# Factorization machine layer: inputs laid out by halves and loaded in fewer pieces

## The chip, the cores and the metric

The kernel runs on one core of a Trainium2 chip. The metric is device time in microseconds (us), the median of several executions. A core has five engines with a queue each: TensorE (PE in the profile, its weight loads are PEld), VectorE (DVE), ScalarE (ACT), GpSimd (POOL) and SyncE (SP). SyncE only issues transfers here; ScalarE and GpSimd issue some too. All transfers are carried out by the core's 16 DMA engines.

## The reference

For a batch x of 1024 rows with 512 features, a weight of shape (64, 512, 512), a linear weight of shape (512, 512) and a bias of 512:

```python
out_lin = x @ lin_w.T + lin_b
xv = jnp.einsum('bf,efm->bem', x, weight)
zp = jnp.einsum('bf,efm->bem', jnp.square(x), jnp.square(weight))
interaction = 0.5 * jnp.sum(jnp.square(xv) - zp, axis=1)
return out_lin + interaction
```

Everything is float32. By far the largest part is xv, 64 products of 1024 x 512 x 512.

## The kernel before

The matrix products are done by Strassen's scheme (Winograd's form), seven products of quarter matrices instead of eight, on two levels. The outer level splits x in four quarters: A11 and A12 are the first 512 rows with one and the other half of the features (k = 0, 1 and k = 2, 3 below), A21 and A22 the other 512 rows. Of these the kernel makes R5 = A22 - A21, R6 = -R5 - A11, R7 = A11 - A21 and R3 = -R6 - A12, and from each of the seven the inner level's sums. All of them stay in one tile, x_all, for the whole run. Then 16 groups of the weight pass by; in each, seven trees (one for each outer product) of seven inner products run on TensorE (`tree`, L603; its matmuls are at L625), while VectorE, ScalarE and GpSimd make the sums of weights and collect the results from PSUM.

Ahead of the groups stands the linear layer, x @ lin_w.T, with one level of the same scheme (`lin_product`, L442; its matmuls are at L458). It runs in the head, while the first inputs arrive. Its seven products come in the order 1, 2, 4, 5, 6, 3, 7. Product 1 (A11 with the first quarter of lin_w) and product 2 (A12) go by k: a feature index is p*4 + k for partition p and k from 0 to 3, so each k is a slab of 128 features, and each slab can be multiplied when it has landed. Product 1 takes k = 0 and 1, product 2 takes k = 2 and 3, and each slab goes by halves of its 512 rows. Product 4 takes A22 and t4, a sum of quarters of lin_w (`column_sums`, L430: t1, t2, t4, t3 in that order on VectorE; t1 and t2 need the second half of lin_w's columns). Product 5 is the first that needs R5, and so A21.

The inputs arrive on two queues. `load_x` (L348) issues pieces of x from SyncE into the tiles oa0 (A11), oa1 (A12), oa2 (A21) and oa3 (A22); `load_lw` (L355) issues pieces of lin_w from the queue that it is given into ob0 (k = 0, 1) and ob1 (k = 2, 3), by halves of the columns (c = 0, 1). In DRAM x is stored transposed, (512, 1024), and so is lin_w: a feature's row of x is 4 KB long, and 2 KB of it belong to one half of the batch. After the inputs SyncE issues the first group's weights w11, w21, w12, w22a (L339).

The order of the work on each engine is written by a planner (`Plan`, L21 to L194) when the kernel is built: each operation has a cost, reads and writes; TensorE's order is given by keys; the other engines take what is ready and most urgent in a simulated time. The loads of the head aren't planned: they are issued as the code has them, and `landing` (L345) only tells the planner at what time, by estimate, their data is there. The compiled program gives each transfer of SyncE and ScalarE one of eight completion semaphores in turn, and a transfer that gets one for the second time first waits until the earlier one has landed.

Later, from the second group to the eighth, `x_squares` (L726) loads quarters of x once more, to square them.

Of the kernel before, what the change touches and what calls it, by code (L numbers as in the profile page):

```python
# [197 lines left out]
def kernel(  # L198
# [38 lines left out]

    nc = tc.nc
    NG, NQ, _, NCB, KH, N = weight.shape
    B = xT.shape[1]  # L240
    M = out.shape[0]
    NB = B // P
    NK = 2 * KH
    MG = M // NG
    MI = MG // 4
    E = N // MI
    H = B // 2
    Q = B // 4

# [10 lines left out]
    buf = {}  # L260
# [32 lines left out]
    bias = sb.tile([P, M // P], F32, tag="bias", name="bias")  # L293
    w2_sum = sb.tile([P, NK, M], F32, tag="w2_sum", name="w2_sum")
    acc_dram = dram.tile([P, M // P, B], F32, tag="accd", name="accd")
    lin_dram = dram.tile([P, M // P, B], F32, tag="lind", name="lind")
    sq_dram = dram.tile([P, 7, 7, Q], F32, tag="sqd", name="sqd")
# [22 lines left out]
    def act(o, i, func, reads, writes, cost=1.04):  # L320
        def emit(_):
            if func is None:
                nc.scalar.copy(o, i)  # L323
            else:
                nc.scalar.activation(o, i, func)  # L325

        plan.add({ACT: cost}, emit, reads, writes)
# [10 lines left out]
    def dma(o, i, reads, writes, move=1.75, on=(SP,)):  # L338
        plan.add(dict.fromkeys(on, 0.45), lambda e: queues[e].dma_start(o, i), reads, writes,  # L339
                 land=2.0, move=move)  # L340


    x_src = xT.rearrange("(p k) b -> p k b", k=NK)
    lw_src = lin_wT.rearrange("(p k) m -> p k m", k=NK)
    def landing(name, at):  # L345
        plan.add({SP: 0.0}, None, (), (name,), land=at - 2 * plan.HOP)

    def load_x(h, k, lo, hi, at):  # L348

        n, r = f"oa{2 * h + k // KH}", k % KH  # L350
        nc.sync.dma_start(buf[n][:, r, lo * Q:hi * Q], x_src[:, k, h * H + lo * Q:h * H + hi * Q])  # L351
        for u in range(lo, hi):
            landing((n, r, u), at)

    def load_lw(queue, ks, c, at):  # L355

        l, r = f"ob{ks[0] // KH}", ks[0] % KH
        queue.dma_start(  # L358
            buf[l][:, r:r + len(ks), ts(c, N // 2)],
            lw_src[:, ks[0]:ks[0] + len(ks), ts(c, N // 2)],  # L360
        )
        for k in ks:
            landing((l, k % KH, c), at)

    load_x(0, 0, 0, 1, 3.5)
    load_lw(nc.scalar, [0], 0, 3.5)
    load_x(0, 0, 1, 2, 3.9)
    load_lw(nc.scalar, [1], 0, 5.2)
    load_x(0, 1, 0, 2, 5.0)
    load_lw(nc.scalar, [2, 3], 0, 7.2)  # L370
    load_x(0, 2, 0, 2, 6.4)
    load_x(0, 3, 0, 2, 7.4)
    load_lw(nc.sync, [0, 1], 1, 8.4)
    load_lw(nc.sync, [2, 3], 1, 9.2)
    for at, k in enumerate((2, 3, 0, 1)):
        load_x(1, k, 0, 2, 10.0 + 0.8 * at)
    nc.scalar.dma_start(bias[:], lin_b)
    landing("bias", 9.5)
    nc.scalar.preload_act_table(AF.Square)


    zero = nc.const_aps.tensor(0.0, [P, N])
# [23 lines left out]
    def x_sum(writes, o, a, b, kind, reads, size, engine=DVE):  # L406

        if kind != "-a - b":
            costs, emit = two_input(engine, o, a, b, kind == "a - b", size)
        else:  # L410
            costs = two_input(DVE, o, a, b, True, size)[0]

            def emit(_):
                nc.vector.scalar_tensor_tensor(o, a, -1.0, b, ALU.mult, ALU.subtract)

        plan.add(costs, emit, reads, writes, both=engine == DVE)
# [285 lines left out]
    def turn(g, tiles, half=True):  # L702

        row = tuple((acc_name[g], i, pos) for i, pos in acc_parts if (i in (2, 3)) + 2 * (i in (4, 5)) & tiles)
        b = {1: slice(0, NB // 2), 2: slice(NB // 2, NB), 3: slice(0, NB)}[tiles]
        a, t = buf[acc_name[g]][:, b, :], buf["turned"][:, b, :]
        size = (b.stop - b.start) / NB
        names = tuple(("turned", h) for h in range(2) if tiles & 1 << h)
        if half:
            plan.add({ACT: 0.2 + 0.25 * size}, lambda _: nc.scalar.mul(a, a, 0.5), row, row)  # L710
        plan.add(
            {DVE: 0.1 + 0.27 * size},
            lambda _: nc.vector.transpose(
                t.rearrange("p n m -> p (n m)"), a.rearrange("p n m -> p (n m)")
            ),
            row, names,
        )
        return b, names
# [7 lines left out]
    def x_squares(i):  # L726

        a, b = c_ring(), c_ring()
        quads = {"A11": (0, 0), "A12": (0, 1), "A21": (1, 0), "A22": (1, 1)}

        def take(o, n):
            if n in raw_dram:
                dma(buf[o], raw_dram[n], (("rawd", n),), (o,))
            else:
                h, q = quads[n]
                dma(buf[o], x_src[:, ts(q, KH), ts(h, H)], (), (o,))
                act(buf[o], buf[o], AF.Square, (o,), (o,), 1.07)

        one, two, kind = {
            1: ("A11", None, None), 2: ("A12", None, None), 4: ("A22", None, None),  # L740
            5: ("A21", "A22", "a + b"), 6: (5, "A11", "a - b"), 7: ("A11", "A21", "a - b"),
            3: ("A12", 6, "a - b"),
        }[i]
        take(a, one)
        if two:
            take(b, two)
            x_sum((a,), buf[a], buf[a], buf[b], kind, (a, b), 1024)
        if i in raw_dram:
            dma(raw_dram[i], buf[a], (a,), (("rawd", i),))
        slots = sq_dram[:, i - 1, 0:4, :].rearrange("p (k q) b -> p k (q b)", k=2)  # L750
        if i in (3, 4, 7):
            return dma(slots, buf[a], (a,), (("sqd", i),))
        a11, a21, a12, a22 = (buf[a][:, k, ts(q, Q)] for k in range(2) for q in range(2))
        s1, s2, s4 = (buf[b].rearrange("p k b -> p (k b)")[:, ts(z, Q)] for z in range(3))
        for o, x, y, kind, to in (
            (s1, a21, a22, "a + b", (b,)),
            (s2, s1, a11, "a - b", (b,)),
            (s4, a12, s2, "a - b", (b,)),
            (a21, a11, a21, "a - b", (a,)),
        ):  # L760
            x_sum(to, o, x, y, kind, (a, b), Q)
        dma(slots, buf[a], (a,), (("sqd", i),))
        dma(sq_dram[:, i - 1, 4:7, :].rearrange("p s b -> p (s b)"),
            buf[b].rearrange("p k b -> p (k b)")[:, 0:3 * Q], (b, ("sqd", i)), (("sqd", i),), 1.3)
# [26 lines left out]
    for g in range(NG - 1):  # L791
        group(g)
        b, names = turn(g, 3)
        m, c = (g * MG) % P, g * MG // P
# [183 lines left out]
    v, o2, u2, f = ("w12", 0), ("w12", 1), ("T1", 0), ("T1", 1)  # L978
# [96 lines left out]
    for i in (7, 4, 3):  # L1075
        if i != 3:
            at = {7: 5, 4: 4}[i]
# [5 lines left out]
    for h in (1, 0):  # L1083
        b, names = turn(last, 1 + h, h == 1)
# [3 lines left out]
    for u, bank in ((1, b2[0]), (0, "b3")):  # L1088
        o = buf[bank][:, u, :]
# [9 lines left out]
    for u, lo, hi, bank, key in ((1, 0, H, "b1", 9.7), (0, 0, Q, b2[1], 14), (0, Q, H, b2[0], 15)):  # L1099
        o = buf[bank][:, 0, 0:hi - lo]  # L1100
# [41 lines left out]
```

## Time and profile before

| | |
|---|---|
| Median of 3 runs | 1403.36 us (1403.36 to 1403.88) |
| The profiled execution | 1404.54 us, of which span 1402.7 us |
| TensorE | 1396.1 us busy, 3296 matmul instructions |
| VectorE, ScalarE, GpSimd | 1093.5, 711.5, 1050.2 us busy |
| Transfers | 211.33 MB, 151 GB/s on average |
| Loads of x in the head, from SyncE | 7 of 256 KB, 2 of 128 KB |
| Loads of lin_w in the head | 3 from ScalarE, 2 from SyncE |

The span goes from the first to the last instruction; the time of an execution lies some 1.8 us above it. A matmul in float32 appears as two instructions with two weight loads. The chain that ended last is followed back from the last instruction, at each step to what released it. An entry such as `[1.32 <-DMA oa<-xT]` says that the engine was idle for 1.32 us before the instruction, and that a transfer from xT into oa ended it. The bound of a stage is read from what ends its waits, not from how busy an engine is over the whole.

### The profile page before, as it was taken

What the parts mean: (1) busy time and instruction counts of PE and PEld (TensorE: products, weight loads), DVE (VectorE), ACT (ScalarE), POOL (GpSimd) and SP (SyncE); (2) the same over time, 40 slices, a digit from 0 to 9 for tenths busy, and PEclk for the clock granted to TensorE, in tenths of its full rate; (3) what the DMA queues carried; (4) which work ended last, traced back from release to release, by engine and by line L of the source; (5) the groups of instructions that cost most, each with busy time, mean ns of one, the idle gap of its engine ahead of it and who ended that gap; (6) DMA issues with size and microseconds to landing.
All of it is one profiled execution on the core that took longest, in us unless ns stands there. A gap on an engine that the chain in (4) does not pass through costs nothing.

```text
span 1402.7 us, 10645 instructions
## 1 busy us (share of the span) xinstructions
PE 1396.1 (100%) x3296; PEld 626.6 (45%) x3296; DVE 1093.5 (78%) x971; ACT 711.5 (51%) x748; POOL 1050.2 (75%) x741
## 2 busy tenths in 40 slices
PE   9999999999999999999999999999999999999998
PEld 4444444444444444444444444444444444444454
DVE  7978696877959778696877959678696877959676
ACT  4546373544736456373544636355373544636444
POOL 4796786958778686786958678686786958678994
PEclk9999999999999999999999999999999999999999
DMA  6674573827649285582827538184472817538363
GB/s 224 165 180 131 124 195 105 230 86 178 200 121 239 85 196 170 125 227 78 228 56 180 154 96 209 45 196 122 127 180 81 227 53 180 153 97 207 101 165 114
DMA packets 54999, 211.33 MB, mean 151 GB/s; under 512 B 21472, under 2 KB 23008, under 8 KB 33056
## 3 DMA queue, kind: packets, MB, share of 16 engines
q0 software_dynamic: 12320, 83.24, 30.8%
q1 hardware_dynamic: 40352, 125.12, 25.3%
q10 hardware_dynamic: 2272, 2.30, 0.5%
q8 instruction: 27, 0.44, 0.1%
q14 instruction: 28, 0.23, 0.1%
HBM read 180.75 MB, written 12.45 MB: 138 GB/s over the span
## 4 chain that ended last, share of the span: by engine, by line
PE 98%; DMA 1%; DVE 0%; ACTq 0%; SPq 0%; DVEq 0%; issue 0%
PE b L625 96%; PE b L458 1%; PE b L936 1%; PE b L1055 1%; DMA ob<-lin_wT 0%; DMA oa<-xT 0%; DVE x_all L311 0%; ACTq L358 0%; SPq L351 0%; DVE T L1034 0%; DVEq L1138 0%; DVE T L1067 0%; DVEq L311 0%
## 5 line engine op out<-in xcount | busy, mean ns | idle before, releaser
L625 PE MATMUL b<-t,x_all 128*128 128x512 f32 x1792 | 806.0, 592 | 0.0
L625 PEld LDWEIGHTS b<-t,x_all 128*128 128x128 f32 x1792 | 340.4, 190 | 427.0 <-issue 420.7
L625 PE MATMUL b<-w,x_all 128*128 128x512 f32 x768 | 358.1, 592 | 0.0
L311 POOL TENSOR_TENSOR t<-w 128x512 f32<-128x512 f32 x128 | 171.9, 1344 | 150.2 <-PE b L625 77.8
L323 ACT COPY p<-b 128x1024 f32<-128x1024 f32 x163 | 164.0, 1006 | 179.3 <-PE b L625 178.5
L625 PEld LDWEIGHTS b<-w,x_all 128*128 128x128 f32 x768 | 145.9, 190 | 183.7 <-issue 182.5
L311 POOL TENSOR_TENSOR t<-w,t 128x512 f32<-128x512 f32 x128 | 175.3, 1370 | 56.7 <-PE b L625 56.5
L325 ACT ACTIVATE oa<-oa 128x1024 f32<-128x1024 f32 x124 | 129.7, 1057 | 145.0 <-DVE oa L311 145.0
L625 PE MATMUL b<-T,x_all 128*128 128x512 f32 x384 | 180.4, 592 | 0.0
L323 ACT COPY b<-b 128x1024 f32<-128x1024 f32 x113 | 112.7, 997 | 133.0 <-PE b L625 132.5
L332 DVE TENSOR_REDUCE acc<-oa 128x16 f32<-128x1024 f32 x124 | 148.8, 1211 | 36.8 <-ACT oa L325 36.8
L332 DVE TENSOR_REDUCE w_sum<-wsq 128x16 f32<-128x1024 f32 x128 | 153.7, 1209 | 3.2 <-ACT wsq L325 3.2
L311 DVE TENSOR_TENSOR oa<-b,p 128x1024 f32<-128x1024 f32 x95 | 115.8, 1219 | 37.2 <-PE b L625 37.2
L325 ACT ACTIVATE c<-c 128x1024 f32<-128x1024 f32 x77 | 79.6, 1055 | 124.3 <-DVE c L311 82.2
L311 POOL TENSOR_TENSOR t<-T 128x512 f32<-128x512 f32 x64 | 86.4, 1350 | 56.6 <-issue 30.9
L625 PEld LDWEIGHTS b<-T,x_all 128*128 128x128 f32 x384 | 73.0, 190 | 91.8 <-issue 90.9
L311 DVE TENSOR_TENSOR p<-b,p 128x1024 f32<-128x1024 f32 x79 | 96.4, 1220 | 20.9 <-PE b L625 16.9
L311 DVE TENSOR_TENSOR ob<-b,p 128x1024 f32<-128x1024 f32 x48 | 58.6, 1222 | 65.8 <-PE b L625 65.8
L325 ACT ACTIVATE wsq<-w 128x1024 f32<-128x1024 f32 x96 | 98.2, 1053 | 12.0 <-DMA w<-weight 9.2
L311 POOL TENSOR_TENSOR t<-T,t 128x512 f32<-128x512 f32 x64 | 82.8, 1293 | 17.8 <-PE b L625 17.7
L311 POOL TENSOR_TENSOR c<-oa,p 128x1024 f32<-128x1024 f32 x32 | 84.7, 2647 | 0.0
L311 DVE TENSOR_TENSOR oa<-b,oa 128x1024 f32<-128x1024 f32 x62 | 75.6, 1219 | 9.5 <-PE b L625 9.5
(100 smaller groups left out, 1394.0 us busy)
## 6 DMA issues: line engine op xcount, KB each, us to landing
w<-weight SPq DMA_DIRECT2D x48, 1024.0 KB, 5.0
T<-weight POOLq DMA_DIRECT2D x45, 1024.0 KB, 9.0
T<-weight SPq DMA_DIRECT2D x30, 1024.0 KB, 6.9
w<-weight POOLq DMA_DIRECT2D x16, 1024.0 KB, 11.1
w<-T POOLq DMA_DIRECT2D x16, 1024.0 KB, 7.0
w22a<-weight SPq DMA_DIRECT2D x8, 1024.0 KB, 10.9
w22b<-weight SPq DMA_DIRECT2D x8, 1024.0 KB, 10.9
c<-xT SPq DMA_DIRECT2D x9, 512.0 KB, 6.1
```

What stands on the lines that cost most here:

```text
L311: f(o, a, b)
L323: nc.scalar.copy(o, i)
L325: nc.scalar.activation(o, i, func)
L332: lambda _: nc.vector.tensor_reduce(o, i.rearrange("p a (m e) -> p a m e", e=E), axis=AX.X, op=ALU.add),
L458: nc.tensor.matmul(buf[bank][:, c, rows], b[:, k, ts(c, P)], a[:, k, rows], start=first and k == 0 and rows.start == 0, stop=k == KH - 1, ...
L625: nc.tensor.matmul(buf[b][:, j, :], buf[f"X{i}"][:, SLOT[p], ts(j, P)], op, start=first, stop=True, skip_group_check=True,)
L936: nc.tensor.matmul(buf[b][:, u, lo:lo + Q], tt[i][p][0], buf[f"X{square_at[i]}"][:, SLOT[p], :], start=first and not lo, stop=True, skip_g ...
L1055: nc.tensor.matmul(o, ap[:, k, ts(u, P)], in_rows(o, buf[raw[i]][:, k, lo:hi]), start=first and k == 0, stop=k == 1, skip_group_check=True,)
```

## The change

x and lin_w are laid out differently in DRAM, on the host: as [half, partition, k, row], where a half is 512 rows of x (or 256 columns of the transposed lin_w). A partition's two k's of one half then lie side by side, and one transfer takes both with rows of 4 KB for x and 2 KB for lin_w. k = 2 and 3 of the first half of x become one load, and the second half of x becomes two (A22, then A21) instead of four. The second half of lin_w's columns is still loaded in two transfers, but from ScalarE's queue, behind the bias and the load of ScalarE's function table; SyncE then issues x alone. The estimates of landing given to the planner change with it. `x_squares` reads from the new layout.

```diff
-    def load_x(h, k, lo, hi, at):
+    def load_x(h, ks, lo, hi, at):
 
-        n, r = f"oa{2 * h + k // KH}", k % KH
-        nc.sync.dma_start(buf[n][:, r, lo * Q:hi * Q], x_src[:, k, h * H + lo * Q:h * H + hi * Q])
-        for u in range(lo, hi):
-            landing((n, r, u), at)
+        n, r = f"oa{2 * h + ks[0] // KH}", ks[0] % KH
+        nc.sync.dma_start(
+            buf[n][:, r:r + len(ks), lo * Q:hi * Q],
+            xT[h][:, ks[0]:ks[0] + len(ks), lo * Q:hi * Q],
+        )
...
+    def load_lw(ks, c, at):
+
+        for q in sorted({k // KH for k in ks}):
+            mine = [k for k in ks if k // KH == q]
+            r = mine[0] % KH
+            nc.scalar.dma_start(
+                buf[f"ob{q}"][:, r:r + len(mine), ts(c, N // 2)],
+                lin_wT[c][:, mine[0]:mine[0] + len(mine), :],
+            )
...
-    load_x(0, 0, 0, 1, 3.5)
-    load_lw(nc.scalar, [0], 0, 3.5)
-    load_x(0, 0, 1, 2, 3.9)
-    load_lw(nc.scalar, [1], 0, 5.2)
-    load_x(0, 1, 0, 2, 5.0)
-    load_lw(nc.scalar, [2, 3], 0, 7.2)
-    load_x(0, 2, 0, 2, 6.4)
-    load_x(0, 3, 0, 2, 7.4)
-    load_lw(nc.sync, [0, 1], 1, 8.4)
-    load_lw(nc.sync, [2, 3], 1, 9.2)
-    for at, k in enumerate((2, 3, 0, 1)):
-        load_x(1, k, 0, 2, 10.0 + 0.8 * at)
+    load_x(0, [0], 0, 1, 3.5)
+    load_lw([0], 0, 3.5)
+    load_x(0, [0], 1, 2, 4.2)
+    load_lw([1], 0, 4.2)
+    load_x(0, [1], 0, 2, 5.2)
+    load_lw([2, 3], 0, 5.8)
+    load_x(0, [2, 3], 0, 2, 7.2)
     nc.scalar.dma_start(bias[:], lin_b)
-    landing("bias", 9.5)
+    landing("bias", 7.2)
+    load_x(1, [2, 3], 0, 2, 9.8)
+    load_x(1, [0, 1], 0, 2, 11.5)
     nc.scalar.preload_act_table(AF.Square)
+    load_lw([0, 1, 2, 3], 1, 8.8)
...
-                dma(buf[o], x_src[:, ts(q, KH), ts(h, H)], (), (o,))
+                dma(buf[o], xT[h][:, ts(q, KH), :], (), (o,))
...
+    def halves(a):
+
+        a = np.asarray(a)
+        return np.ascontiguousarray(a.reshape(2, a.shape[0] // 2, p, n_k).transpose(0, 2, 3, 1))
+
     arrays = {
-        "xT": np.ascontiguousarray(np.asarray(r_x).T),
+        "xT": halves(r_x),
...
-        "lin_wT": np.ascontiguousarray(np.asarray(L0_rec_lin_w).T),
+        "lin_wT": halves(L0_rec_lin_w),
```

## The prediction

> **What bounds the kernel now.** I read the page's first lines, then the waits of TensorE over the whole span, then the chain that ended last, and last the first 17 us engine by engine.
>
> ```profile
> span 1402.7 us, 10645 instructions
> PE 1396.1 (100%) x3296; PEld 626.6 (45%) x3296; DVE 1093.5 (78%) x971; ACT 711.5 (51%) x748; POOL 1050.2 (75%) x741
> ```
>
> TensorE has work throughout. Its complete list of waits in the whole run has three entries:
>
> ```profile
> PE b L458 <- DMA oa<-xT: 1.3, 1, 1.3
> PE b L384 <- PEq L1131: 0.8, 1, 0.8
> PE b L458 <- DVE x_all L311: 0.7, 1, 0.7
> ```
>
> Two of them are at L458, the matmuls of the linear layer, so both lie in the head. The 0.8 is the start of the program. The chain, in order of time, shows where the head ends (start, length, what; pieces left out at "..."):
>
> ```profile
> 1.67 6.55 DMA ob<-lin_wT
> 8.22 0.02 issue
> 8.24 0.34 SPq L351
> ...
> 9.10 6.12 DMA oa<-xT
> 15.21 0.03 issue
> ...
> 15.34 1.24 DVE x_all L311
> 16.57 0.04 issue
> 16.62 12.28 PE b L458 x28
> 28.90 1.72 PE b L625 x4
> 30.62 1.72 PE b L458 x4
> 32.33 1323.55 PE b L625 x3084
> ```
>
> From 16.62 us on the chain is TensorE back to back until 1398.03: 1381.4 us in which loads don't matter as long as they keep their cover. The end of the run is therefore 16.62, the start of product 5 (the first that needs R5 = A22 - A21), plus a constant. Only what moves that start counts. TensorE up to there (start, busy, instructions, idle before):
>
> ```profile
> 3.48 2.25 PE L458 MATMUL b<-oa,ob 128*128 128x256 f32 x8
> 7.04 5.42 PE L458 MATMUL b<-oa,ob 128*128 128x256 f32 x24 [1.32 <-DMA oa<-xT]
> 12.30 3.60 PE L458 MATMUL b<-oa,p 128*128 128x512 f32 x8
> 16.62 7.13 PE L458 MATMUL b<-x_all,p 128*128 128x512 f32 x16 [0.72 <-DVE x_all L311]
> ```
>
> k-step 0 is done at 5.73; k-step 1 waits for x's k=1 (landed 6.91); k=1, 2, 3 run until 12.2 (24 x 0.215); product 4 runs 12.30 to 15.73 (8 x 0.429). Then 0.89 us without work (the view says 0.72, its ends being modelled). Two holes, 1.31 and 0.89: 2.2 us in all. That is the whole stake, 0.16%.
>
> Why A21 is late is in the queue's own waits:
>
> ```profile
> SPq L351 <- DMA ob<-lin_wT: 3.8, 2, 3.0
> ```
>
> [...] The second load of x's second half thus waited 3.0 us for lin_w's [2,3], which landed at 8.22; the last two went out at 8.62 and 9.06. The trace's completion records of the last (A21's k=1): fifteen of its sixteen engines had landed by 12.74, the sixteenth at 15.21.
>
> **What the Trainium skill says.** "DMA: Bandwidth & Descriptors", section "Why a DMA increments its semaphore by 16 and not by 1": a transfer is finished when all its engines are. The 12.74 against 15.21 agrees. Section "Queues, rings and completion order": an engine takes the rings in turns by packets, and descriptors of one ring start in order, so what lies ahead on the same ring is paid first; lin_w's [2,3], third on its queue, took 6.6 us beside x's pieces, which agrees. Section "Why small descriptors are slow (HBM only)": a fixed cost per packet. The packet records agree: 1 KB took 46 ns, 2 KB 84, 8 KB 309, that is 37 ns per KB and about 9 per packet. Section "Issuing engines are not separate DMA queues": moving a load between queues saves issue time only; here 0.33 to 0.47 us each.
>
> **The change part by part.**
>
> Longer rows. Per engine (8 of the 128 rows of each transfer): before 16x46 ns for the two first pieces of x, 7x8x84 for the others, 64x46 for lin_w: 0.74+4.70+2.94 = 8.38 us. After: 0.74 + 8x84 + 3x8x159 for x (4 KB: 84 plus 2x37 = 158 to 159, an estimate from the three sizes), and 16x46 + 24x84 for lin_w: 0.74+0.67+3.82+0.74+2.02 = 7.98. So 0.40 us less wire, all before A21's end.
>
> Issue. SyncE issued 11 transfers before the weights, now 6. Four go at 0.75 to 2.5 (0.43 each). A22 is now the ninth and waits for lin_w's first (landed 3.34): out at 3.36 instead of 4.71 and 8.24. A21 waits for the third of x's and lin_w's first four (3.87): out at 3.9 instead of 8.62 and 9.06. The 3.0 us wait is gone from x and falls on w11, now the thirteenth, which waits for lin_w's [2,3]. Before, w11 went out at 9.57 and landed at 17.98; TensorE's first use is at 28.7, through a sum on GpSimd that starts at 18.05 and takes under 2 us, so some 8 us of cover. I count it as nothing; a weight later than that would cost the excess.
>
> A21's landing. A21's first half landed at 12.10 before, with 7.7 us of packets ahead of and in it: 12.10-1.5-7.7 = 2.9 us over pure packet time (first packet 1.5; waits, slow first reads, receipt). The same on 7.98: 1.5+7.98+2.9 = 12.4. Below: 10.2[...]; above: 14.9 if one engine lags by 2.5 again. Needed: product 4's end 15.73 less R5's 1.24 and 0.09 of hops = 14.4. At 12.4, R5 waits for VectorE instead: its sums of lin_w, then the 1.22 us addition into ob2 that ended at 13.79; so R5 13.8 to 15.05, product 5 at 15.73. **The hole of 0.89 goes.**
>
> k-step 1. x's k=1 keeps its place, third on SyncE's queue, and its issue time. lin_w's [2,3] beside it moves 2 KB packets instead of 1 KB: in turns, 8x(84+84) = 1.34 instead of 8x(84+46) = 1.04, so up to 0.3 later; with both started earlier by nothing, at best as much earlier as less queueing gives. From -0.4 (it landed on twelve engines by 5.38) to +0.3; I take 0. A delay goes one to one into product 5; a gain does too, if VectorE keeps up.
>
> k-steps 2, 3. They were due at 8.77 and 10.5; x's pieces landed at 8.03 and 8.81, lin_w's at 8.22. Now both k's of x are one 512 KB transfer, issued at 2.1 (before: 2.1 and 3.3), needed whole at 8.77. Cover 0 to 0.7: I take 0, bound +1.5.
>
> lin_w's second half. Issued from SyncE at 3.73 and 4.20, landed 9.51 and 10.18. Now behind bias and the table load on ScalarE (2.67 + 1.28 = 3.95), so 3.95 and 4.4: 0.2 later, but on the other ring than x's. VectorE makes t1, t2, t4 from it, 3x0.69, the last done at 12.03 for product 4 at 12.2. Cover 0.2; cost 0, bound +0.7. Queued behind these issues on ScalarE is only x's first copy, at 7.01.
>
> Squares' loads of x later (nine of 512 KB, now 4 KB rows) lie under TensorE's 1381 us. TensorE's order is unchanged; VectorE, ScalarE and GpSimd swap neighbours in places because the planner's landing times differ. TensorE had no wait in the body, so these cost nothing unless a slack is used up: 0, bound +1.
>
> Sum: -0.89. For the profiled execution, 1404.54 (span 1402.7 and 1.84 around it), that makes 1403.65 and a span of 1401.8; the median of the runs is 1.18 below its own profile, so 1403.36-0.89 = **1402.5**.
>
> **Rivals.** *Hidden anyway* (0.20): the sixteenth engine's lag may belong to that one execution, 1.2 us longer than the median. Without it A21 was in by 12.74 in time, product 5 already follows product 4, and nothing is gained: 1403.4. Against: such a lag shows on the weight w12 too (fifteen engines at 21.64, the last at 23.23). *Both holes close* (0.07): k-step 1 starts with step 0's end as well: 1403.36-2.2 = 1401.2, if VectorE's sums move too; against, the transfer that it waits for isn't moved. *The early second half crowds the first* (0.14), the other side: A22, A21 and lin_w's rest, 1.5 MB, enter the engines at about 4.5 to 5.5, while x's [2,3] needs 8.77. If it gets half the turns, 8x159 becomes 2.5 us and with slow engines it ends at 10.5: 1.7 late, less the 0.89: +0.8, 1404.2. It decides from 8.77+0.89 = 9.66 on; +2.8 would take a landing at 12.5. *A stall in the body* through the changed order, some 3 us, 1406: 0.02.
>
> **How the numbers follow.** Forecast 0.57, its own range 1402.1 to 1403.0. 0.2% of this kernel is 2.8 us, about what a measurement can tell from no change, and more than both holes: faster by that needs something not in the sum, 0.01. Slower: the tail of the crowding and the body, 0.05. Same 0.94. The range takes in half of "both holes" and the crowding up to its price: 1401.3 to 1404.3.
>
> **What would show it.** Right: TensorE's wait for VectorE at L458 gone or under 0.2, product 5 near 15.7, no wait of SyncE for lin_w longer than about 1 us among x's loads, A21 landed by 13, TensorE's wait at k-step 1 still 1 to 1.6. Wrong: a new wait of L458 for x or lin_w at 8.8 to 10 or at 12.2, or any TensorE wait after 17 us.

## The result: slower by 0.5%

The changed kernel takes 1409.87 us (median of 6 runs, 1408.19 to 1413.51) against 1403.5 us before (6 runs, 1403.33 to 1404.18): a ratio of 1.005, 95% interval 1.0037 to 1.0064. I had forecast 1402.5, in a range of 1401.3 to 1404.3; the result lies above it.

The profile after is of its fastest run, 1408.19 us with a span of 1406.4. TensorE's list of waits, which had three entries, now reads:

```profile
PE b L460 <- DVE p L311: 1.7, 1, 1.7
PE b L460 <- DMA ob<-lin_wT: 0.9, 1, 0.9
PE b L386 <- PEq L1139: 0.8, 1, 0.8
PE b L460 <- DVE x_all L416: 0.2, 1, 0.2
```

L460 is the linear layer (L458 before). The wait for R5 is gone, as foretold; in its place stands a wait for "p", the tile with VectorE's sums of lin_w (t1 to t4). TensorE in order of time (start, busy, instructions, idle before):

```profile
4.55 9.71 PE L460 MATMUL b<-oa,ob 128*128 128x256 f32 x32 [0.87 <-DMA ob<-lin_wT]
16.01 3.70 PE L460 MATMUL b<-oa,p 128*128 128x512 f32 x8 [1.75 <-DVE p L311]
19.54 3.60 PE L460 MATMUL b<-x_all,p 128*128 128x512 f32 x8
23.39 3.67 PE L460 MATMUL b<-x_all,p 128*128 128x512 f32 x8 [0.24 <-DVE x_all L416]
```

Three things are to be seen. The first matmul starts at 4.55 instead of 3.48. Products 1 and 2 then have no hole, that is no idle time, but take 9.71 us for 32 instructions, which at 0.215 us each would be 6.9. The clock record of this profile begins only at 9.72 (before: at 4.12), and up to there TensorE is at half its clock: it works at 12 of these instructions in the 5.1 us from 4.6 on, and at 21 in the 4.2 us from 9.8 on. And product 4 starts at 16.01 instead of 12.30. Product 5 follows at 19.54 instead of 16.62. VectorE shows what product 4 waited for:

```profile
11.00 0.69 DVE L311 TENSOR_TENSOR p<-ob 128x512 f32<-128x512 f32 x1
14.54 1.42 DVE L311 TENSOR_TENSOR p<-ob,p 128x512 f32<-128x512 f32 x2 [2.85 <-DMA ob<-lin_wT]
```

t1 is done at 11.7; t2, and t4 behind it, wait 2.85 us for the last piece of lin_w, which landed at 14.44 (before: 10.18). ScalarE's queue issued the two pieces of lin_w's second half here:

```profile
3.60 2.29 ACTq L362 DMA_DIRECT2D ob<-lin_wT  x2
```

The body is unchanged to the hundredth: the chain's longest piece, TensorE at L627, is 1323.55 us long as before. It starts at 35.78 instead of 32.33, so 3.45 of the 3.7 us by which this span is longer are lost ahead of it, and nearly all of that in the first 24 us: product 6 starts 3.3 us later than it did (23.39 against 16.62 and the 3.43 of product 5).

### The profile page after: what moved, and what is told of

The parts are those of the page before. It is cut to its first block, busy times and chain, and to the rows that moved or that the text cites. A ratio compares the mean times of both kernels' runs of the same rounds, so it can differ in the third digit from the quotient of the medians.

```text
span 1406.4 us, 10634 instructions
## 1 busy us (share of the span) xinstructions
PE 1398.7 (99%) x3296; PEld 628.0 (45%) x3296; DVE 1093.2 (78%) x971; ACT 711.9 (51%) x748; POOL 1047.7 (74%) x741
## 4 chain that ended last, share of the span: by engine, by line
PE 98%; DMA 1%; DVE 0%; issue 0%; ACTq 0%; DVEq 0%
PE b L627 96%; PE b L938 1%; PE b L460 1%; PE b L1057 1%; DMA w<-weight 1%; DMA ob<-lin_wT 0%; DVE x_all L416 0%; DVE x_all L311 0%; DVE ob L506 0%; ACTq L362 0%; DVE p L311 0%; DVE T L1036 0%; DVEq L1146 0%; DVE T L1069 0%; DVEq L311 0%
## 5 line engine op out<-in xcount | busy, mean ns | idle before, releaser
L627 PE MATMUL b<-t,x_all 128*128 128x512 f32 x1792 | 806.0, 592 | 0.0
L627 PEld LDWEIGHTS b<-t,x_all 128*128 128x128 f32 x1792 | 340.4, 190 | 427.0 <-issue 418.8
L627 PE MATMUL b<-w,x_all 128*128 128x512 f32 x768 | 358.1, 592 | 0.0
L627 PEld LDWEIGHTS b<-w,x_all 128*128 128x128 f32 x768 | 145.9, 190 | 183.7 <-issue 182.0
L627 PE MATMUL b<-T,x_all 128*128 128x512 f32 x384 | 180.4, 592 | 0.0
L627 PEld LDWEIGHTS b<-T,x_all 128*128 128x128 f32 x384 | 73.0, 190 | 91.8 <-issue 89.0
```

The source lines that it names most:

```text
L627: nc.tensor.matmul(buf[b][:, j, :], buf[f"X{i}"][:, SLOT[p], ts(j, P)], op, start=first, stop=True, skip_group_check=True,)
```

## Where a longer execution loses more

Five of the six runs are 1.6 to 5.3 us longer than the profiled one, with a mean granted clock of 0.997 or 0.998. So one more execution of the changed kernel was profiled.

> The changed kernel once more, for the profile of another execution. If it is a longer one (1409.5 or more): the clock falls to half once in the head after its first rise, and the hole before product 4 is over 1.75 us. If it is as short as the first profile: as that one.

It took 1411.68 us, span 1409.9. Its chain, in order of time:

```profile
1.19 4.29 DMA ob<-lin_wT
5.48 0.02 issue
5.50 10.39 DMA ob<-lin_wT
15.89 0.03 issue
...
15.98 0.70 DVE p L311
16.69 0.02 issue
16.71 1.65 DVE p L311
18.36 0.04 issue
18.40 17.41 PE b L460 x36
```

This chain leads to the late start of product 4. The last piece of lin_w is issued only at 5.50, because its semaphore was last used by lin_w's k = 1, which landed at 5.48 (4.08 before). It is under way for 10.4 us. By then w11 has landed too (16.21), and GpSimd begins its sums:

```profile
16.28 3.19 POOL L311 TENSOR_TENSOR t<-w 128x512 f32<-128x512 f32 x2 [15.83 <-DMA w<-weight]
```

VectorE's t4 beside it takes 1.65 us instead of 0.69. TensorE stands idle for 4.79 us, and its clock falls. The windows of this execution (window, its length, busy time of PE, PEld, VectorE, ScalarE and GpSimd, then PEclk, the third number from the right, the DMA share and GB/s):

```profile
10.00:18.00 8.00, 3.61 (x17) 2.85 (x15) 3.69 (x6) 2.90 (x4) 1.72 (x2) 1.00 1.04 422
18.60:21.90 3.30, 3.30 (x5) 1.24 (x5) 3.30 (x3) 0.00 (x0) 3.30 (x3) 0.50 0.90 375
22.00:26.00 4.00, 4.00 (x11) 1.82 (x10) 4.00 (x3) 1.27 (x2) 4.00 (x3) 1.00 0.39 154
```

By the clock records it is at half from 18.53 to 21.94, 3.41 us, just as product 4 runs at last; from its start to that of product 5, product 4 takes 5.24 us instead of 3.43. Product 5 starts at 23.64, 7.0 later than before, and the span is 7.1 longer. This expectation held.

The Trainium skill describes this in "TensorE: Matmul & The Clock Gate", Part 1: TensorE's clock is halved after an idle window of about 3.4 us and comes back after a busy one, and the windows run freely and do not start anew with a kernel. The records agree on the length: the falls in the head last 3.41, 6.83 and 10.24 us, one, two and three such windows, and each begins three or four windows (10.24 or 13.65 us) after the rise. They differ in one point: a window needn't be idle throughout. Counted in windows of 3.41 us from each profile's first rise, TensorE was busy for 0, 0.13, 0.37, 0.56 and 1.00 us in the five windows of the head that ended in a fall, and for 1.67 us or more in all other windows of the head at full clock (by the modelled ends of the matmuls); 1.67 is the first profile, whose hole of 1.75 us brought no fall. So where a hole lies in a window counts as well as its length. The first rise goes the same way: it came with the end of windows in which TensorE was busy for 2.88 us or more, and not after 2.86 or less (2.54 in the first profile, with the hole of 0.87 us ahead of its first matmul).

## Experiments

All are compared with the kernel before on the same chip, whose median was 1403.4 to 1403.8 each time. Two theories stood at the start. **Ring** (a queue's list of packets at each DMA engine): lin_w's second half travels in 1 KB packets on ScalarE's ring and gets one turn against each larger packet of SyncE's ring. **Layout**: the new layout makes the first reads slow, so TensorE's first matmul comes late and its clock with it.

### Queues alone, layout alone

Queues alone is the old layout with the new pieces, order and queues (against the changed kernel; parts are left out at "..." here and below):

```diff
-            xT[h][:, ks[0]:ks[0] + len(ks), lo * Q:hi * Q],
+            x_src[:, ks[0]:ks[0] + len(ks), h * H + lo * Q:h * H + hi * Q],
...
-                lin_wT[c][:, mine[0]:mine[0] + len(mine), :],
+                lw_src[:, mine[0]:mine[0] + len(mine), ts(c, N // 2)],
...
```

> The old layout in DRAM with the new pieces, order and queues (x in rows of 2 KB). Ring theory (the second half of lin_w goes in packets of 1 KB on ScalarE's ring and gets one turn against each larger packet of SyncE): most of the loss is here, 1406 to 1410 us, the second half of lin_w lands at 12.5 to 14 us, product 4 waits for VectorE's sums. Layout theory (the new layout makes the first reads slow, so TensorE's warm-up ends before data is there and its clock rises at 9.7 instead of 4.1): nothing is lost here, 1403 to 1404, first piece of lin_w at 3.4, clock up at 4.1.

Measured: 1407.05 us, ratio 1.0025 (1.0015 to 1.0035). The first piece of lin_w landed at 3.38, the last at 12.52, and TensorE waits where the ring theory says:

```profile
14.09 3.70 PE L462 MATMUL b<-oa,p 128*128 128x512 f32 x8 [1.53 <-DVE p L311]
...
22.31 3.67 PE L462 MATMUL b<-x_all,p 128*128 128x512 f32 x8 [0.80 <-DVE x_all L418]
```

Product 4 is 1.8 late. Product 6 waits too: GpSimd starts its sums at 15.41 (before: 18.05), and R5 and R7 beside them take 4.28 us on VectorE instead of 2.36.

Layout alone is the new layout with the old calls (against the kernel before):

```diff
-        nc.sync.dma_start(buf[n][:, r, lo * Q:hi * Q], x_src[:, k, h * H + lo * Q:h * H + hi * Q])
+        nc.sync.dma_start(buf[n][:, r, lo * Q:hi * Q], xT[h][:, k, lo * Q:hi * Q])
...
-            lw_src[:, ks[0]:ks[0] + len(ks), ts(c, N // 2)],
+            lin_wT[c][:, ks[0]:ks[0] + len(ks), :],
...
```

> The new layout with the old pieces, order and queues. Ring theory: 1403 to 1404, second half of lin_w by 10.2 us. Layout theory: first pieces later (lin_w's first at 4.5 instead of 3.3), clock up at 9.7, 1405 to 1410.

Measured: 1405.19 us (1403.13 to 1407.55), ratio 1.0011 (1.0003 to 1.002). So both theories hold a part. lin_w's first piece landed at 4.28; 143 packets of data started between 3 and 4 us, against 226 before, and took 87 ns on average against 66. The profiled execution was the fastest, and its clock was up at 3.8, so it doesn't show the loss: its span, 1401.3, is below the 1402.7 before.

### lin_w's second half back on SyncE

```diff
-            nc.scalar.dma_start(
+            queue.dma_start(
...
+    load_lw([0, 1, 2, 3], 1, 8.8, nc.sync)
     load_x(1, [2, 3], 0, 2, 9.8)
     load_x(1, [0, 1], 0, 2, 11.5)
     nc.scalar.preload_act_table(AF.Square)
-    load_lw([0, 1, 2, 3], 1, 8.8)
```

> The changed kernel, but the second half of lin_w back on SyncE's queue, behind x's first half and ahead of its second. Ring theory: it lands by 10.5 us, product 4 follows product 2 without a wait, 1402.5 to 1404. Layout theory: the late clock stays, and with it 1405 to 1408.

Measured: 1405.79 us, ratio 1.0014 (1.0007 to 1.0022), with the last piece of lin_w landing at 10.51 and no wait for "p". This takes back 4.1 of the 6.4 us. What is left goes with the other theory, by the profile, which is of the slowest of its runs: first matmul at 5.01, the clock up at 10.0, and then product 6 waiting 0.81 us for a sum that VectorE makes beside GpSimd:

```profile
5.01 9.64 PE L460 MATMUL b<-oa,ob 128*128 128x256 f32 x32 [1.33 <-DMA ob<-lin_wT]
...
22.52 3.67 PE L460 MATMUL b<-x_all,p 128*128 128x512 f32 x8 [0.81 <-DVE x_all L416]
```

### Warm-up lengthened

Ahead of the first product TensorE multiplies constants, to be busy until data is there; the widths of these matmuls stand in one line. One more of them, in the changed kernel:

```diff
-    for width in (N, N // 2):
+    for width in (N, N // 2, N // 2):
```

> The changed kernel with one more warm-up matmul of 256 columns, which keeps TensorE busy until about 4.6 us. Ring theory: the clock is up early and products 1 and 2 end earlier, but product 4 still starts near 16 us: no gain, 1407 to 1411. Clock theory (the late clock is what costs): 1403 to 1405.5.

Measured: 1411.36 us, ratio 1.0055 (1.004 to 1.007). As the ring theory said, no gain: the clock is up at 5.9 and product 2 done by 13.75, and product 4 starts at 16.20 all the same. Then the clock falls, from 16.16 to 19.58:

```profile
16.20 5.36 PE L460 MATMUL b<-oa,p 128*128 128x512 f32 x8 [2.45 <-DVE p L311]
```

The same edit in the kernel with the layout alone:

> The new layout with the old pieces, order and queues, and one more warm-up matmul of 256 columns (TensorE busy to about 4.6 us). Clock theory (the new layout costs because the first piece comes after the warm-up has ended, and the clock then comes up a whole period later in many executions): median falls from 1405.2 to 1402.5 to 1404 and the spread of 4.4 us narrows to under 2. If the late first pieces cost by themselves, through k-step 1: it stays at 1405.

Measured: 1403.23 us, ratio 1.0001 (0.9992 to 1.001). The layout's 1.7 us are gone with 0.9 us of matmuls on constants, although lin_w's first piece still landed at 4.58. The lines of both kernels, layout alone first:

```profile
4.32 1.99 PE L456 MATMUL b<-oa,ob 128*128 128x256 f32 x8 [0.64 <-DMA ob<-lin_wT]
```

```profile
4.62 7.52 PE L456 MATMUL b<-oa,ob 128*128 128x256 f32 x32
```

The first has a hole ahead of it, the second none. As the data come no earlier, the late pieces must cost here through TensorE's hole, and so through the clock's rise; that is inferred, since no slow execution of the layout alone was profiled. The opposite edit, in the kernel before:

```diff
-    for width in (N, N // 2):
+    for width in (N,):
```

> The kernel before without the second warm-up matmul: TensorE's warm-up ends near 2.8 us and some 0.7 us pass before the first piece is there. Clock theory: the clock comes up later in many executions, 1404.5 to 1406.5, spread over 2 us. Otherwise nothing changes: 1403.5.

Measured: 1404.02 us, ratio 1.0004 (0.9995 to 1.0013), less than I expected and not clear of nothing. Its profile has the clock up at 8.3 instead of 4.1, with a hole of 0.56 before the first matmul, so a late rise alone costs little in the old layout.

### Which array's layout

Each array alone in the new layout, with the old calls (the diff is the half of the layout edit that concerns it).

> The kernel before with x alone in the new layout (lin_w in the old one). If x's layout makes the first reads slow: first piece of lin_w at 4.2 or later, 1404.5 to 1406. If lin_w's layout does: first piece at 3.4, 1403 to 1404.

> The kernel before with lin_w alone in the new layout (x in the old one). If lin_w's layout makes the first reads slow: its first piece lands at 4.2 us or later, TensorE waits for it after the warm-up, and in many executions the clock is late: 1404.5 to 1406. If only both layouts together do: 3.4 and 1403.5.

Measured: x alone 1403.51 us, lin_w alone 1403.53, both ratio 1.0002 (0.9993 to 1.001). lin_w's first piece landed at 3.38 and 3.65, against 4.17 to 4.97 in all nine profiles that have both. So neither array alone costs time. Its second piece (k = 1) shows that each alone slows the first reads somewhat: 4.08 before, 4.37 to 4.75 with one new layout, 5.33 to 5.77 with both. Why is not settled: nothing here shows how the two layouts meet in memory.

### The queue again, with rows of 4 KB

The changed kernel with lin_w in the old layout, once with its second half on ScalarE and once on SyncE, ahead of x's second half. Nothing differs between the two but that queue and the place in it.

> The changed kernel with lin_w in the old layout; against the run with queues and pieces alone it differs in x's rows, 4 KB instead of 2. If the rings take turns by packets: the second half of lin_w lands later than the 12.5 us of that run, at 13.3 or later, product 4 starts at 15 or later, 1408 to 1410. If turns go by bytes or only the time of issue counts: 12.5, 14.1 and 1407.

> The changed kernel with lin_w in the old layout and its second half on SyncE ahead of x's second half. If the ring and the late first pieces of the two new layouts together are all of the loss: 1403 to 1404.2, first piece of lin_w by 3.5, x's k = 1 by 7.2. If the 4 KB rows or the merged pieces of x cost by themselves: 1405.

Measured: 1412.47 us (1.005, interval 1.0034 to 1.0067) on ScalarE, 1403.83 us (0.9999, interval 0.9991 to 1.0008) on SyncE. The queue of two 256 KB loads is worth 8.6 us here. In the old layout the same move costs 3.0 us (1407.05 for queues alone against the 1404.01 of the new pieces alone, below), in the changed kernel 4.1. On ScalarE the last piece landed at 15.76, and t2 and t4 beside GpSimd's sums took 3.38 us instead of 1.41; this is the profile:

```profile
15.85 3.38 DVE L311 TENSOR_TENSOR p<-ob,p 128x512 f32<-128x512 f32 x2 [3.66 <-DMA ob<-lin_wT]
...
19.29 5.97 PE L462 MATMUL b<-oa,p 128*128 128x512 f32 x8 [7.04 <-DVE p L311]
```

The ring theory had 1408 to 1410; the slow sums, and the clock (below), come on top. On SyncE the last piece landed at 10.42:

```profile
9.22 3.69 PE L462 MATMUL b<-oa,ob 128*128 128x256 f32 x16 [0.58 <-DMA oa<-xT]
12.75 3.67 PE L462 MATMUL b<-oa,p 128*128 128x512 f32 x8
```

The 0.58 is a wait for x's merged k = 2 and 3, which landed at 9.09; it leaves no trace in the median. With x in rows of 2 KB (queues alone, on ScalarE) lin_w's last piece landed at 12.52. The packet records show turns: between 10 and 11 us, 79 packets of 4 KB of x and 79 of 1 KB of lin_w started in the changed kernel, a fifth of the bytes for lin_w (78 and 86 in its longer execution). Later its last packets stand against weights of 8 KB. The kernel on ScalarE has two groups of runs, 1406.9 and 1407.6, and four from 1412.4 to 1413.1; the profiled one is of the second group, with the clock at half from 17.1 to 23.9.

### The new pieces alone

The old layout with the new pieces, and lin_w's second half on SyncE; and the same with a tiny copy on GpSimd that reads R6 ahead of its sums:

```diff
+    plan.add({POOL: 0.1}, lambda _: nc.gpsimd.tensor_copy(hold[:], x_all[:, 5, 0, 0:1]), ("R6",), ("hold",))
...
```

> The old layout with the new pieces, and lin_w's second half on SyncE ahead of x's second half. Neither the slow first reads nor the ring are in it. The prediction's own mechanism (A21 earlier, product 5 follows product 4): 1402.5. Collision theory (the weights come earlier too, GpSimd's sums start near 15.5 us and make VectorE's R5, R7 and R6 slower, so product 6 waits some 0.8 us): 1403 to 1404.

> As the run with the old layout, the new pieces and lin_w's second half on SyncE, with one tiny copy on GpSimd ahead of its sums that waits for R6. Collision theory: R5, R7 and R6 take 1.22 us each, product 6 doesn't wait, 0.5 to 0.9 us faster than without the hold, 1402 to 1403. Otherwise: the same as without, or slower if GpSimd's later start reaches TensorE.

Measured: 1404.01 us (1.0004, interval 0.9996 to 1.0013) and 1403.82 us (1.0002, interval 0.9993 to 1.001). In both profiles product 5 follows product 4 at 15.7, as I had forecast (the first of the two):

```profile
15.68 7.03 PE L462 MATMUL b<-x_all,p 128*128 128x512 f32 x16
```

and there is still no gain. In the second, R6 took 1.22 us (2.29 without the hold), but product 6 didn't wait in either. The collision of VectorE with GpSimd costs nothing here; product 6 waited for it in queues alone (0.80 us) and in the changed kernel with lin_w on SyncE (0.81), where R5 came later.

### Both repairs, and the hole filled

The changed kernel with lin_w's second half on SyncE and the longer warm-up:

> The changed kernel with both repairs: lin_w's second half on SyncE ahead of x's second half, and one more warm-up matmul of 256 columns. If the ring and the clock are all of the loss: 1403 to 1404.3. If something else is left: 1405 or more.

Measured: 1404.98 us, ratio 1.001 (1.0001 to 1.0018). 1.6 us are left: the queue and the clock are not all of the loss. TensorE's one long wait says where:

```profile
8.24 5.54 PE L460 MATMUL b<-oa,ob 128*128 128x256 f32 x24 [1.58 <-DMA oa<-xT]
```

x's k = 1 landed at 8.10 instead of 6.91, now with the clock up and TensorE waiting for data. With the layout alone it landed at 6.48 and 6.55; it is late, 7.14 to 8.20, in all seven profiles that have both layouts and the new pieces, and why these add up is not settled. The kernel with lin_w in the old layout on SyncE, above, has it at 6.40 and loses nothing. So taking back the queue and one of the two layouts takes back the whole loss, with the new pieces and x's rows of 4 KB kept.

To test the clock in the hole I put two matmuls on constants between products 2 and 4, first with their cost told to the planner, then without:

> The changed kernel with two matmuls on constants between products 2 and 4, 1.7 us in the hole where TensorE waits for lin_w's second half. If the clock drops in that hole in most executions and this is the rest of the loss: median falls from 1409.9 to 1407.5 to 1408.8, mean clock at 0.999 or more. If not, or if the fill only delays product 4: 1410 to 1411.

> The changed kernel with two matmuls on constants between products 2 and 4 that the planner doesn't know of, so that the orders stay. If the clock drops in the hole in most executions and this is the rest of the loss: median falls from 1409.9 to 1407.5 to 1408.8, mean clock 0.999 or more. If the hole is long in most executions because the second half of lin_w comes later still, filling 1.7 us of it doesn't keep the clock: 1409 to 1411.

Measured: 1416.02 us and 1412.91 us, both above what either side expected. The first decides nothing: the planner, given 1.7 us more for TensorE, put t4 behind t3 and another sum on VectorE. In the second the orders are unchanged, but lin_w's last piece landed at 16.58, product 4 started at 19.69, and the clock fell to half at 20.1 for 3.4 us all the same: the hole behind the fill was still 3.7 us. What the fall costs was not isolated by an experiment; in the profile of the longer execution it goes with 1.8 us more in product 4.

## Why the prediction was wrong

**lin_w's second half (cost 0, bound +0.7) is the step that failed.** It has three errors. I took the other ring for harmless or better, although I had quoted that engines take rings in turns by packets: on SyncE's ring the piece stood ahead of x's second half and of the weights, on ScalarE's it had to share with all of them, 1 KB against 4 and 8. The other sentence that I had quoted, that moving a load between queues saves issue time only, does not hold here: the move cost 3.0 to 8.6 us. I gave its packets 2 KB, the length of the rows at the source; the destination tile holds two halves of the columns side by side, and the records show 1024 packets of 1 KB on ScalarE's ring, all of lin_w. And I put its issue at 4.4, while its semaphore belongs to lin_w's k = 1, which held it until 5.5. Bound +0.7, measured: product 4 late by 3.7 us in one profile and 6.1 in the other, though in the first TensorE itself was late, by about 2, and waited only 1.75. Put back on SyncE, 4.1 of the 6.4 us are gone. The other 2.3 belong to the next two terms.

**Longer rows (-0.40 us of wire).** lin_w's part of it, 2.94 to 2.76, doesn't exist. For x the 4 KB packet took 159 ns, the estimate. But I priced packets at their median and took the first reads of the new layout to be as quick as those of the old: they were not. A21 landed at 13.45, not at 12.4.

**k-step 1 (0, from -0.4 to +0.3).** x's k = 1 landed 0.8 later (7.69), and the late first piece moved the clock's rise. My sum had no term for the clock, though k-step 0 before runs at half of it until 4.1 us; the warm-up matmuls ahead of it were in the code.

**The hole of 0.89 goes.** It does, and gives nothing: the rival "hidden anyway" was right. Five further profiles with the old order of loads (layout alone, the same with the warm-up, x alone, lin_w alone, the short warm-up) have A21 landed by 12.55 to 13.88, and none of them waits for R5. None has the sixteenth engine's lag to 15.21, which I had seen in one execution, 1.2 us above the median. My sum then took its hole off the median, which most likely never had it: 1403.36 less 1.84 and less the 1386.1 from product 5's start to the end puts that start at 15.4 in the median execution (an estimate), ahead of the 15.7 that I forecast.

**The weights (counted as nothing).** I asked only whether they would be late. The first, w11, was early, 16.05 and 16.21 instead of 17.98: this brought 8 KB packets against lin_w's and, in the longer execution, GpSimd's sums onto VectorE's t4. By itself it costs nothing: with lin_w in the old layout on SyncE it landed at 15.62.

**The rival on the other side** had the right kind of mechanism, loads that start earlier and crowd one that is needed, at the wrong place. x's [2,3] landed at 9.56 and TensorE, still at half clock, didn't wait for it; lin_w's second half was crowded. (With lin_w in the old layout on SyncE, TensorE did wait for it, 0.58 us at 9.22.) **The body** was right: no wait after 24 us. Of the signs of being right, three failed: product 5 near 15.7 (19.54), A21 by 13 (13.45), and no wait of SyncE for lin_w over 1 us among x's loads (2.0). Of the signs of being wrong, the wait ahead of product 4 came.

## What to carry to other kernels

On one ring the order of issue was also the order of arrival in the head of all 18 profiles; moving a load to another queue gives that order up, and a load with small packets then gets the smaller share of the bytes. Before loads are started earlier, ask whom they will crowd, and check the contiguous run on both sides before counting on longer rows. And where TensorE's first microseconds bound the end, a hole can cost more than its length, because the clock may come up later or fall: count that too. Last, trust a hole that one profile shows only when a second one shows it, and don't subtract one execution's hole from the median of the runs.

## What the runs showed of the hardware

- Ring turns go by packet: 79 of 4 KB against 79 of 1 KB in one microsecond.
- Two layouts that each cost no time (first piece of lin_w at 3.38 and 3.65 us) were slow together (4.17 to 4.97).
- Half clock for 3.41 us in or after holes of 2.45 us (the changed kernel with the longer warm-up), 3.7 (the unplanned fill) and 4.8 (the longer execution); for 6.83 us with the hole of 7.0 (rows of 4 KB, on ScalarE); for 10.24 with one of 7.6 (the planned fill). None with holes of 1.5 us (queues alone) and 1.75 (the first profile after).
- Beside GpSimd's sums, an addition of 512 elements a partition took VectorE 1.75 us (t3 in the longer execution) instead of 0.68.
